# Seven chunks instead of three gather raw rows, and 13 blocks of normalised rows are turned in three rounds, in a two-layer graph network on Trainium2

## The chip, the cores and the metric

The kernel runs on one core of a Trainium2 chip. The metric is the device time of one launch in microseconds (us), taken as the median of several runs; lower is better. The core has TensorE (PE, with PEld for its weight loads), VectorE (DVE), ScalarE (ACT), GpSimd (POOL) and SyncE (SP), and 16 DMA engines that all of them issue to.

## The reference

A graph of 6250 nodes with 128 features each has 106250 edges (50000 random pairs in both directions and a loop for each node), sorted by destination. Two transformer convolutions with two heads of 64 run after each other; all of it is in f32. The features of an edge, `e`, come from a cosine time encoding (32) and a message (64).

```python
kj    = k[src] + e                            # k, q, v: linear maps of h
alpha = einsum('ehc,ehc->eh', q[dst], kj) / sqrt(C)
a     = softmax of alpha over the edges of one dst
conv(h) = segment_sum((v[src] + e) * a, dst) + h @ Ws + bs

h = conv1(x)
h = relu(batchnorm(h))                        # mean and variance over all 6250 nodes
out = layernorm(x + conv2(h))
```

The batch norm stands between the layers: its mean and variance are complete only when layer 1 has given its last rows. Per feature it becomes a scale and a shift.

## The kernel before

**Tiling.** The edges are cut into `NC` = 105 chunks of up to 1024 edges (`T` = 8 tiles of 128), each for at most 64 consecutive destinations. A chunk's features lie in a tile `ff` (an edge per partition and tile). The feature rows of its sources are fetched by eight indirect DMAs of 128 rows each, issued by GpSimd (`gather`, L752): from `xv_d` in layer 1, and in layer 2 from one of two tables in DRAM. `h_d` holds the raw rows of layer 1's result, `hn_d` the same rows after batch norm and relu.

**Layers.** `conv(c, extra, first_blocks)` runs once for each layer (c = 0 and 1), as one loop over rounds k from -4 to 107 with the order of instructions written out by hand (L948 and on). Every engine works through its own instructions in that order and waits for the others by semaphores. Round k issues, in this order:

- `fetch(k+4)`: SP loads the messages (`fmsg`), the tables of scores (`ftab`) and, in layer 2, the encodings (`fz`), their turned copies (`fxT<-et_d`) and the residual rows (`fr`); then `gather(k+4)` on GpSimd.
- `score(k, 0)` (L831, L832), `turn_weights(k-1)` (L856 on TensorE, copied by ScalarE at L857), `divide(k-2)` on VectorE (L868 to L871), `score(k, 1)`, `lowest(k)` (L838, L840), `finish_turn(k-2)` (TensorE turns the divided sums, L883 and L884; VectorE copies them, L886).
- `turn_in(k+1, 0)`: TensorE turns half of the next chunk's rows (L806), ScalarE copies the result out of PSUM: in layer 2 with scale, shift and relu if the rows are raw (L811), as they are otherwise (L813).
- `gather_sums(k-1)`: eight matmuls (L863) that sum the weighted rows by destination, the last readers of the chunk's `ff`. Then `weigh(k)` (ScalarE, L846), `turn_in(k+1, 1)`, `apply(k-2)` (L899, L900 in layer 2), and `settle(k+2)`, a copy of messages.
- `pull(extra)`: a step or two of work from a generator. In layer 2 these are, for one block of 512 nodes after the other, the tables of scores (L630 on TensorE, copied by ScalarE and VectorE) and the residual `x + h @ Ws + bs` (L1093).
- `finish(k-2)`, `normalise(k)` if the chunk's rows are raw, the copy of the encodings into `ff` (L997), and the store of results.

**Buffers.** `ff` has six, `fmsg` three, `fz` four; so the gather of chunk k+6 can begin only when the sums (L863) of chunk k are done. PSUM has three banks for everything that is turned (tag "tr", with the blocks of nodes below), three for scores, one for sums and one for results. The tiles of rows on their way to DRAM (`fhr`, `fxr`) share three buffers.

**Raw rows.** A chunk k < `RAW` in layer 2 gathers from `h_d`, which is complete when layer 1 is. Its turned rows get scale, shift and relu from ScalarE on the way out of PSUM (L811); the untransposed rows, which L863 needs, get them on VectorE:

```python
def normalise(k):
    rows = ch[k].f[:, :, 1:1 + D]
    for i, op in enumerate((OP.mult, OP.add)):                 # L876
        nc.vector.tensor_tensor(rows, rows, pl.spread[:, None, i].to_broadcast([P, T, D]), op)
    nc.vector.tensor_scalar(rows, rows, 0.0, None, op0=OP.max) # L877
```

All later chunks gather from `hn_d` and need none of this, but the first of them must wait until all of `hn_d` is stored.

**Between the layers.** VectorE forms scale and shift from the statistics (L1067 to L1077), ScalarE does the relu of the first block of `hT` (the 6250 nodes as columns, in SBUF), the tables and the residual of that block are made, and scale and shift are spread over all partitions (L1122 to L1128). Then `conv(1, ...)` begins. In its first round, k = -4, right after `fetch(0)` and `gather(0)`, it calls `first_blocks`: ScalarE does relu of blocks 1 to 12 in place (L1107), and for each of the 13 blocks TensorE turns four tiles of 128 nodes (L1028), VectorE copies them out of PSUM (L1030) and SP stores them to `hn_d` (L1038; the last block is 106 rows and goes in two stores, L1043; 14 stores in all).

Of the kernel before, what the change touches and what calls it, by code (L numbers as in the profile page):

```python
# [7 lines left out]
F32 = mybir.dt.float32  # L8
# [5 lines left out]
P = 128  # L14
# [4 lines left out]
TD = 32  # L19
# [3 lines left out]
GE = GT * P  # L23
# [21 lines left out]
T = 8  # L45
# [618 lines left out]
def ordered(ctx: ExitStack, tc: tile.TileContext, pl, x, dst, edge_attr_64, conv2, bn_g, bn_b, out):  # L664
# [3 lines left out]
    N = x.shape[0]  # L668
# [19 lines left out]
    def first(k):  # L688
        return max(0, N - NN * (NC - k)), min(N - 1 if k == NC - 1 else N - NN, NN * k)
# [6 lines left out]
    AHEAD = 4  # L696

    SINGLE = 40

    RAW = 3  # L700

    def conv(c, extra, first_blocks=None):

# [2 lines left out]
        load = cs.enter_context(tc.tile_pool(name=f"fload{c}", bufs=AHEAD + 2))  # L706
# [16 lines left out]
        def fetch(k):  # L723
            s = ch[k] = Plan()
            lo, hi = first(k)
            s.nb = nc.sync.value_load(pl.nbs[0:1, k:k + 1], min_val=lo, max_val=hi)
            sl = nc.sync.value_load(pl.sls[0:1, k:k + 1], min_val=0, max_val=E - CE)
            s.f = f = load.tile([P, T, FW], F32, name="ff")
            s.msg = load.tile([P, T, MSG], F32, name="fmsg", bufs=3)
            nc.sync.dma_start(s.msg, edge_attr_64[bass.ds(sl, CE), :].rearrange("(p t) d -> p t d", t=T))  # L730
            if c:
                nc.vector.memset(f[:, :, D + EW:1 + D + EW], 1.0)
            else:
                bits = small.tile([P, T, BITS], I32, name="fbits")
                nc.vector.tensor_tensor(bits, pl.dsts[:, :, k:k + 1].to_broadcast([P, T, BITS]),
                                        pl.bitm[:, None, :].to_broadcast([P, T, BITS]), OP.bitwise_and)
                nc.vector.tensor_scalar(f[:, :, D + EW:D + EW + BITS], bits, 0.0, None, op0=OP.is_equal)
                nc.vector.tensor_copy(f[:, :, D + EW + BITS:], bits)
            s.tab = load.tile([P, NN * H, 3 - c], F32, name="ftab")
            nc.sync.dma_start(s.tab, pl.tab_d[c][:, bass.ds(s.nb, NN)].rearrange("p n h w -> p (n h) w"))  # L740
            if c:
                s.z = load.tile([P, T, TD], F32, name="fz", bufs=AHEAD)
                nc.sync.dma_start(s.z, enc_d[k].rearrange("p (t d) -> p t d", d=TD))
                s.et = ets[k % len(ets)]
                nc.sync.dma_start(s.et, et_d[k])
                s.r = load.tile([NN, D], F32, name="fr", bufs=AHEAD + 3)
                nc.sync.dma_start(s.r, res_d[bass.ds(s.nb, NN), :])

        def gather(k):
            f = ch[k].f  # L750
            ch[k].rows = [
                nc.gpsimd.indirect_dma_start(  # L752
                    out=f[:, t, (1 if c else 0):1 + D], out_offset=None, in_=(h_d if k < RAW else hn_d) if c else pl.xv_d,
                    in_offset=bass.IndirectOffsetOnAxis(ap=pl.srcs[:, t, k:k + 1], axis=0))
                for t in range(T)]
# [24 lines left out]
        def sine():  # L780
            arg, *of = args
            args.clear()
            z = work.tile([P, 2, T, TD], F32, name="fzs")
            nc.scalar.activation(z[:, :len(of)], arg[:, :len(of)], AF.Sin, bias=qpi)
            turned.extend((k, z[:, i]) for i, k in enumerate(of))
# [11 lines left out]
        def turn_in(k, u):  # L797
# [7 lines left out]
            for t in range(4):  # L805
# [3 lines left out]
                s.rows = []  # L809
            if c and k < RAW:  # L810
                nc.scalar.activation(s.ft[:, u * GE:(u + 1) * GE], px, AF.Relu, bias=pl.shift, scale=pl.scale)  # L811
# [11 lines left out]
        def score(k, u):  # L823

            s = ch[k]
            if u == 0:
                s.ps = []
            ps = p_s.tile([P, GE], F32, name="fps")
            s.ps.append(ps)
            w = slice(u * GE, (u + 1) * GE)  # L830
            nc.tensor.matmul(ps, s.tab[:, :, 0], s.ft[:, w], start=True, stop=False)  # L831
            nc.tensor.matmul(ps, s.tab[:EC, :, 1], s.et[:, w], start=False, stop=True)  # L832
# [110 lines left out]
        def pull(gen, n):  # L943
            for _ in range(n):
                next(gen, None)

        with cs, tc.manual_schedule():
            for k in range(-AHEAD, NC + 3):  # L948
                def on(j):
                    return 0 <= j < NC  # L950

                if on(k + AHEAD):
                    fetch(k + AHEAD)
                    gather(k + AHEAD)
                if k == -AHEAD and c:
                    first_blocks()
                if on(k):
                    score(k, 0)
                if on(k - 1):
                    turn_weights(k - 1)  # L960
                place()
                if on(k - 2):
                    divide(k - 2)
                if on(k):
                    score(k, 1)
                if on(k):
                    lowest(k)
                if on(k - 2):
                    finish_turn(k - 2)
                if on(k + 1):  # L970
                    turn_in(k + 1, 0)
                if on(k - 1):
                    gather_sums(k - 1)
                if on(k):
                    weigh(k)
                if on(k + 1):
                    turn_in(k + 1, 1)
                if on(k - 2):
                    apply(k - 2)
                if on(k + 2):  # L980
                    settle(k + 2)
                for j in (k + 2,) if k < SINGLE else (k + 2, k + 3) if k == SINGLE else (k + 3,):
                    if c == 0 and on(j):
                        encode(j)
                        if j < SINGLE + 3:
                            sine()
                if k >= 0:
                    at_round[0] = k
                    pull(extra, 2 if k < 4 or k > 96 else 1)
                if on(k - 2):  # L990
                    finish(k - 2)
                if len(args) == 3 or args and k == NC - 4:
                    sine()
                if c and on(k):
                    if k < RAW:
                        normalise(k)
                    nc.vector.tensor_copy(ch[k].f[:, :, 1 + D:1 + D + TD], ch[k].z)  # L997
                for _ in range(min(len(done), 2 if k > NC - 12 else 1)):
                    store(*done.pop(0))
            at_round[0] = 2 * NC  # L1000
            for _ in extra:
                pass
            for rows in done:
                store(*rows)


    NT = NP // GE

    with tc.tile_pool(name="fpw", bufs=2) as pw:
# [96 lines left out]
            r = slice(b0 * GE, (b0 + 1) * GE)  # L1106
            nc.scalar.activation(hT[:, r], hT[:, r], AF.Relu, bias=shift, scale=scale)  # L1107

        def first_blocks():

            for b0 in range(1, NT):
                relu(b0)
            for b0 in range(-(-N // GE)):
                put_rows(hn_d, b0, turned_rows(b0))

        with tc.tile_pool(name="fpp2", bufs=3, space=bass.MemoryType.PSUM) as pp, tc.manual_schedule():
# [262 lines left out]
```

## Time and profile before

| | before |
|---|---|
| time, median of 3 runs | 2705.21 us (2699.31 to 2705.34) |
| the profiled execution: its own time | 2727.81 us |
| its span in the trace | 2725.5 us |
| instructions | 38782 |
| VectorE, ScalarE, GpSimd busy | 49%, 45%, 59% of the span |
| gathers of layer 1 and layer 2 (L752) | 840 of 958 ns and 840 of about 951 ns |
| moved by DMA | 393.39 MB, mean 144 GB/s |

The times come from the chip's profiler, from one execution; the runs that give the median are others. An engine is busy when one of its instructions executes; waiting, register and DMA-issuing instructions don't count. In the lists of instructions, "x" is a count of equal instructions in a row, and the brackets hold the idle time of that engine before the instruction and what ended it: another instruction or a transfer by its tile, "issue" where the trace shows nothing that it waited for, "remote" where the event that released it has no work of this core's trace beside it. An arrow `out<-in` names the tile written and the tiles read, and what stands before "L" and a number is the engine, after it the line of the kernel.

### The profile page before, as it was taken

How to read it: one execution, taken by the hardware profiler on the slowest of the kernel's cores; microseconds unless marked ns; L12 is line 12 of the kernel's file. 1: busy time of each engine (PE TensorE's matmuls, PEld its weight loads, DVE VectorE, ACT ScalarE, POOL GpSimd, SP SyncE). 2: the span in 40 equal slices, each digit the busy share in tenths (PEclk: the TensorE clock that was granted, in tenths of full speed). 3: DMA queues.
4: the chain of work that ended last, by engine and by line, in shares of the span. 5: the costliest groups of instructions: out<-in, count | busy, mean ns of one | idle time of the engine just before them, and what ended most of it. 6: DMA issues, size and time to landing. Idle time of an engine off the chain costs nothing. (4 is left out here: it accounts for less than half of the span.)

```text
span 2725.5 us, 38782 instructions
## 1 busy us (share of the span) xinstructions
PE 2315.9 (85%) x11482; PEld 1703.1 (62%) x11482; DVE 1332.0 (49%) x4144; ACT 1231.3 (45%) x2147; POOL 1608.2 (59%) x1701
## 2 busy tenths in 40 slices
PE   4599899999898888888956888888988888988887
PEld 3366666667666666666734666666666666656655
DVE  5266666666666666666634333333333333333333
ACT  2266666665554555545522333333333343433344
POOL 3466666566666666666336666666666666666660
PEclk8699999999999999999978999999999999999999
DMA  6255555445544455445436554545555555554440
GB/s 204 76 152 161 160 151 162 123 150 158 161 150 136 150 161 159 143 142 145 127 107 175 157 152 132 160 143 156 155 144 146 159 151 147 150 140 129 139 132 29
DMA packets 239223, 393.39 MB, mean 144 GB/s; under 512 B 62049, under 2 KB 156893, under 8 KB 235677
## 3 DMA queue, kind: packets, MB, share of 16 engines
q1 hardware_dynamic: 166302, 237.60, 28.5%
q0 software_dynamic: 54144, 112.01, 16.2%
q10 hardware_dynamic: 18558, 41.20, 4.1%
q8 instruction: 97, 1.59, 0.2%
q14 instruction: 122, 0.99, 0.1%
HBM read 274.66 MB, written 112.55 MB: 142 GB/s over the span
## 5 line engine op out<-in xcount | busy, mean ns | idle before, releaser
L752 POOL DMA_INDIRECT ff<-xv_d,fsrcs x840 | 804.8, 958 | 511.9 <-issue 212.4
L752 POOL DMA_INDIRECT ff<-hn_d,fsrcs x816 | 775.8, 951 | 466.0 <-issue 208.0
L813 ACT COPY fft<-fpx 128x512 f32<-128x512 f32 x414 | 243.7, 589 | 1124.5 <-remote 459.8
L863 PE MATMUL fpa<-ff,fpt 128*128 128x225 f32 x3360 | 677.4, 354 | 3.5 <-issue 3.5
L863 PEld LDWEIGHTS fpa<-ff,fpt 128*128 128x128 f32 x3360 | 621.6, 190 | 8.0 <-issue 4.7
L838 DVE TENSOR_REDUCE flow<-fps 128x1 f32<-128x512 f32 x420 | 283.4, 686 | 516.7 <-PE fpx L806 167.9
L831 PE MATMUL fps<-fft,ftab 128*128 128x512 f32 x840 | 473.5, 647 | 46.3 <-ACT fft L813 34.5
L856 PEld LDWEIGHTS fppt<-fident,fs 128*128 128x128 f32 x1680 | 200.5, 145 | 145.8 <-issue 75.8
L857 ACT COPY fpt<-fppt 128x512 f32<-128x512 f32 x420 | 227.6, 585 | 119.9 <-issue 46.1
L846 ACT ACTIVATE fs<-fps,fm 128x512 f32<-128x512 f32 x420 | 266.6, 689 | 5.7 <-DVE fm L840 3.3
L806 PE MATMUL fpx<-fident,ff 128*128 128x128 f32 x1680 | 256.2, 276 | 9.4 <-issue 5.0
L856 PE MATMUL fppt<-fident,fs 128*128 128x128 f32 x1680 | 233.7, 283 | 13.0 <-ACT fft L811 5.5
L831 PEld LDWEIGHTS fps<-fft,ftab 128*128 128x128 f32 x840 | 168.0, 234 | 107.4 <-ACT fft L813 53.4
L832 PE MATMUL fps<-fet,ftab 112*128 112x512 f32 x420 | 220.4, 606 | 16.7 <-issue 16.7
L832 PE MATMUL fps<-fxT,ftab 112*128 112x512 f32 x420 | 230.8, 632 | 2.5 <-DMA fxT<-et_d 2.5
L806 PEld LDWEIGHTS fpx<-fident,ff 128*128 128x128 f32 x1680 | 200.6, 142 | 40.5 <-issue 27.6
L818 PE MATMUL fpe<-fident,ff 128*112 128x128 f32 x840 | 131.5, 280 | 60.9 <-ACT fft L813 54.7
L886 DVE COPY fat<-fpo 128x256 f32<-128x256 f32 x210 | 88.4, 421 | 177.6 <-remote 66.6
L832 PEld LDWEIGHTS fps<-fet,ftab 112*128 112x128 f32 x420 | 105.8, 252 | 95.5 <-issue 93.6
L832 PEld LDWEIGHTS fps<-fxT,ftab 112*128 112x128 f32 x420 | 89.5, 213 | 114.1 <-issue 109.4
L819 ACT COPY fet<-fpe 112x512 f32<-112x512 f32 x210 | 126.1, 601 | 55.2 <-remote 17.6
L818 PEld LDWEIGHTS fpe<-fident,ff 128*112 128x112 f32 x840 | 93.7, 135 | 78.3 <-ACT fft L813 69.1
(217 smaller groups left out, 2382.7 us busy)
## 6 DMA issues: line engine op xcount, KB each, us to landing
fmsg<-in_edge_attr SPq DMA_DIRECT2D x210, 256.0 KB
et_d<-fet SPq DMA_DIRECT2D x105, 448.0 KB
fxT<-et_d SPq DMA_DIRECT2D x105, 448.0 KB
ftab<-tab_d SPq DMA_DIRECT2D x105, 192.0 KB
tab_d<-fo ACTq DMA_DIRECT2D x13, 1536.0 KB
ff<-xv_d,fsrcs POOLq DMA_INDIRECT x840
enc_d<-fzs SPq DMA_DIRECT2D x105, 128.0 KB
ftab<-tab_d SPq DMA_DIRECT2D x105, 128.0 KB
```

The source lines that it names most:

```text
L752: nc.gpsimd.indirect_dma_start(out=f[:, t, (1 if c else 0):1 + D], out_offset=None, in_=(h_d if k < RAW else hn_d) if c else pl.xv_d, in_o ...
L806: turn = nc.tensor.transpose(px[:, t * P:(t + 1) * P], s.f[:, u * 4 + t, 1:1 + D], ident)
L813: nc.scalar.copy(s.ft[:, u * GE:(u + 1) * GE], px)
L818: nc.tensor.transpose(pe[:EC, t * P:(t + 1) * P], s.f[:, u * 4 + t, 1 + D:], ident)
L819: nc.scalar.copy(s.et[:, u * GE:(u + 1) * GE], pe[:EC])
L831: nc.tensor.matmul(ps, s.tab[:, :, 0], s.ft[:, w], start=True, stop=False)
L832: nc.tensor.matmul(ps, s.tab[:EC, :, 1], s.et[:, w], start=False, stop=True)
L838: nc.vector.tensor_reduce(low[:, u:u + 1], s.ps[u], AX.X, OP.min)
L846: nc.scalar.activation(s.s[:, u * GE:(u + 1) * GE], s.ps[u], AF.Exp, bias=s.bias, scale=-1.0)
L856: nc.tensor.transpose(pp[:, t * P:(t + 1) * P], s.s[:, at:at + P], ident)
L857: nc.scalar.copy(s.pt[:, u * GE:(u + 1) * GE], pp)
L863: nc.tensor.matmul(s.pa, s.pt[:, t * P:(t + 1) * P], s.f[:, t, 1:1 + D + EW], start=t == 0, stop=t == T - 1)
```

## The change

`RAW` goes from 3 to 7: chunks 0 to 6 gather from `h_d` and are normalised on the fly, and chunk 7 is the first to gather from `hn_d`. `first_blocks` no longer runs at the start of layer 2. It takes the round as its argument and is called at the end of rounds 0, 1 and 2, ahead of the pulled work: four relus each (blocks 4k+1 to 4k+4), and then the blocks 0 to 4 in round 0, 5 to 8 in round 1 and 9 to 12 in round 2 are turned, copied and stored. The gather of chunk 7 is issued at the start of round 3, behind these stores. The encodings `fz` get a fifth buffer.

```diff
-    RAW = 3
+    RAW = 7
...
-                s.z = load.tile([P, T, TD], F32, name="fz", bufs=AHEAD)
+                s.z = load.tile([P, T, TD], F32, name="fz", bufs=AHEAD + 1)
...
                 if on(k + AHEAD):
                     fetch(k + AHEAD)
                     gather(k + AHEAD)
-                if k == -AHEAD and c:
-                    first_blocks()
                 if on(k):
                     score(k, 0)
...
+                if c and k in range(3):
+                    first_blocks(k)
                 if k >= 0:
                     at_round[0] = k
                     pull(extra, 2 if k < 4 or k > 96 else 1)
...
-        def first_blocks():
-
-            for b0 in range(1, NT):
+        def first_blocks(k):
+
+            for b0 in range(4 * k + 1, 4 * k + 5):
                 relu(b0)
-            for b0 in range(-(-N // GE)):
+            for b0 in range(4 * k + (k > 0), 4 * k + 5):
                 put_rows(hn_d, b0, turned_rows(b0))
```

## The prediction

> **What bounds the kernel now.** I read the busy times of the engines first, then the same busy times by stretches of time, then the instructions in order of time where the stretches look unlike the rest. The columns of the stretches are the stretch, its length, busy time (and instructions) of TensorE, weight loads, VectorE, ScalarE and GpSimd, the granted TensorE clock, the DMA share and GB/s.
>
> ```profile
> PE 2315.9 (85%) x11482; PEld 1703.1 (62%) x11482; DVE 1332.0 (49%) x4144; ACT 1231.3 (45%) x2147; POOL 1608.2 (59%) x1701
> ...
> 1400.00:1420.00 20.00, 3.76 (x20) 2.72 (x20) 1.79 (x3) 2.31 (x4) 15.09 (x16) 0.63 0.53 153
> ...
> 1437.80:1455.00 17.20, 14.54 (x49) 8.80 (x47) 7.13 (x14) 7.08 (x9) 13.17 (x14) 0.80 0.70 192
> 1455.00:1472.60 17.60, 4.46 (x6) 1.71 (x6) 0.51 (x2) 2.06 (x4) 9.99 (x11) 0.73 0.28 88
> ...
> 1600.00:1700.00 100.00, 87.49 (x445) 63.36 (x443) 36.23 (x118) 34.18 (x75) 62.22 (x66) 0.97 0.51 148
> ```
>
> TensorE is the busiest engine, 87 of 100 us in a steady stretch of layer 2. Between the layers it is not: it works 3.8 us of the 20 from 1400, and 4.5 us of the 17.6 from 1455. The change acts on this stretch alone. The order of time there (start, length, engine, line, and in brackets the idle time before and what ended it):
>
> ```profile
> 1390.05 0.94 POOL L752 DMA_INDIRECT ff<-h_d,fsrcs  x1 [58.19 <-DVE fshift L1077]
> ...
> 1400.47 1.53 PE L1028 MATMUL fpg<-fident,fhT 128*128 128x128 f32 x12 [0.59 <-DVE fspread L1128]
> ...
> 1406.43 0.69 DVE L1030 COPY fhr<-fpg 128x512 f32<-128x512 f32 x1 [6.02 <-issue]
> ...
> 1413.41 0.69 DVE L1030 COPY fhr<-fpg 128x512 f32<-128x512 f32 x1 [6.28 <-remote]
> ...
> 1418.76 0.94 POOL L752 DMA_INDIRECT ff<-h_d,fsrcs  x1 [0.30 <-issue]
> 1421.81 0.69 DVE L1030 COPY fhr<-fpg 128x512 f32<-128x512 f32 x1 [7.71 <-remote]
> ...
> 1432.01 0.66 PE L806 MATMUL fpx<-fident,ff 128*128 128x128 f32 x4 [0.58 <-DMA hn_d<-fhr]
> ...
> 1437.87 0.94 POOL L752 DMA_INDIRECT ff<-hn_d,fsrcs  x1 [18.17 <-DMA hn_d<-fhr]
> ...
> 1452.57 0.69 DVE L838 TENSOR_REDUCE flow<-fps 128x1 f32<-128x512 f32 x1 [2.81 <-remote]
> ...
> 1462.50 0.78 ACT L811 ACTIVATE fft<-fpx,fshift,fscale 128x512 f32<-128x512 f32 x1 [14.94 <-issue]
> ...
> 1467.09 0.94 POOL L752 DMA_INDIRECT ff<-hn_d,fsrcs  x1 [0.30 <-issue]
> ...
> 1472.47 0.78 ACT L811 ACTIVATE fft<-fpx,fshift,fscale 128x512 f32<-128x512 f32 x1 [8.04 <-remote]
> ...
> 1472.65 0.94 POOL L752 DMA_INDIRECT ff<-hn_d,fsrcs  x1 [4.61 <-remote]
> ...
> 1484.60 0.94 POOL L752 DMA_INDIRECT ff<-hn_d,fsrcs  x1 [1.80 <-PE fpo L900]
> ...
> 1496.72 1.11 POOL L752 DMA_INDIRECT ff<-hn_d,fsrcs  x1 [2.20 <-PE fpx L806]
> ```
>
> Three things are to be seen. The gathers of chunks 0 to 2 run without a break, one every (1418.76 - 1390.05) / 23 = 1.248 us; chunk 3 waits until 1437.87 for the last stored block; chunk 6 starts at 1472.65, chunk 7 at 1484.60, and then a chunk takes 12.1 us. Second, chunk 0's rows lie there from about 1390.05 + 8 x 1.248 = 1400, but TensorE turns them at 1432.01, behind the 13 blocks. Third, the blocks are not slow by their own work: three blocks' transposes were issued by 1402.0, and VectorE takes them up at 1406.4, 1413.4 and 1421.8, that is 7.0 and 8.4 us apart. The last of these is the first after the gathers ended. While gathers run for long, TensorE's results reach the other engines late; I call that holding. Between 1452.57, 1462.50 and 1472.47 it is again 9.9 and 10.0 us, late in the second run of gathers (chunks 3 to 5, 1437.87 to 1468.03). What causes it the profile does not say. It is there in the start of layer 1 too, where six chunks are gathered without a break, as layer 2 will do after the change:
>
> ```profile
> 40.53 0.96 POOL L752 DMA_INDIRECT ff<-xv_d,fsrcs  x1 [25.40 <-PE fpx L654]
> ...
> 69.00 0.58 ACT L813 COPY fft<-fpx 128x512 f32<-128x512 f32 x1 [6.76 <-remote]
> ...
> 80.14 0.58 ACT L819 COPY fet<-fpe 112x512 f32<-112x512 f32 x1 [10.55 <-remote]
> ...
> 91.34 0.58 ACT L813 COPY fft<-fpx 128x512 f32<-128x512 f32 x1 [10.62 <-remote]
> ...
> 99.32 0.94 POOL L752 DMA_INDIRECT ff<-xv_d,fsrcs  x1 [0.30 <-issue]
> ...
> 101.83 0.58 ACT L819 COPY fet<-fpe 112x512 f32<-112x512 f32 x1 [9.91 <-issue]
> ...
> 109.86 1.91 PE L630 MATMUL fpg<-fxT,fm 128*128 128x512 f32 x2
> ...
> 125.08 0.97 POOL L752 DMA_INDIRECT ff<-xv_d,fsrcs  x1 [24.82 <-PE fpa L863]
> ```
>
> There a result is taken up every 10.5 to 11.2 us until the gathers stop at 100.3, and chunk 6 follows 24.8 us after that.
>
> **The change, part by part.** I count to the gathers of chunks 6 and 7 and the sums (L863) that free their buffers, since from there on a chunk costs 12.1 us in both kernels.
>
> *Blocks leave the front.* 49 transposes, 13 copies, 12 relus and 14 stores go; TensorE can turn chunk 0 at about 1402 instead of 1432.0, 30 us earlier. SP no longer has 14 stores between the loads of chunk 0 and those of chunks 1 to 4.
>
> *Raw rows for seven chunks.* Six feature buffers let chunks 0 to 5 be gathered in one run: 1390.05 + 48 x 1.248 = 1450.0. TensorE has rows from 1400 on, but holding starts about then: at 8.4 us a result (the same place, the value nearest to the middle of 7.0 and 11.2) 48 us pass 5.7 results. Chunk 0 needs two turned halves and two score halves, chunk 1 two turned halves: six. So at 1450 chunk 0 is scored and chunk 1 nearly turned; layer 1 is at that point at 109.86 and starts chunk 6 at 125.08, 15.2 us later. If nothing were held it would be done long before 1450; if 11.2 held, two results are missing and layer 1's whole 24.8 us apply.
>
> *Blocks at the ends of rounds 0, 1, 2* (five, four, four). The nearest rows:
>
> ```profile
> L1107 ACT ACTIVATE fhT<-fhT,fshift,fscale 128x512 f32<-128x512 f32 x13 | 9.5, 799 | 2.2 <-DVE fdiag L1126 1.3 <-DVE fshift L1077 0.8
> ...
> L1030 DVE COPY fhr<-fpg 128x512 f32<-128x512 f32 x12 | 8.1, 690 | 24.3 <-remote 14.0 <-issue 6.0 <-DMA hn_d<-fhr 2.8
> ...
> 1424.65 2.34 DMA hn_d<-fhr
> ...
> 2669.61 3.21 PE L863 MATMUL fpa<-ff,fpt 128*128 128x225 f32 x16
> ...
> 2678.90 3.21 PE L863 MATMUL fpa<-ff,fpt 128*128 128x225 f32 x16
> ```
>
> Four copies are 4 x 0.69 = 2.8 us; with three buffers and 2.34 us until a store lands, (0.69 + 0.39 + 2.34) / 3 = 1.14 us a block, 4.6 us for four; four relus 3.2 us on ScalarE ahead of the table copies and of the next round's turned weights. A round's blocks so cost 2.8 to 4.6 us; beside the gathers' gap they might cost nothing. I take 3, for round 0's five 4. Chunk 6 then starts at 1450.0 + 15.2 + 4 = 1469.2, 3.5 us earlier than 1472.65. Round 1 takes 12.1 + 3: its sums are done at 1484.3, 0.3 earlier than 1484.60. Round 2 adds 3.
>
> *Chunk 7 waits for the last block.* Before, its gather needs only the free buffer. Now POOL also waits for round 2's stores, which come behind four relus (3.2), the last copy (0.7) and the landing (2.3) and some transposes: 7 us, from 5.5 to 10. Behind that wait stand all later gathers; TensorE waits for none of them for three rounds. While POOL stands still a round is faster: at the end of layer 2, where nothing is gathered, 2678.90 - 2669.61 = 9.3 us instead of 12.1, which gives back up to 2.8; I take 2.4. The 7 us late gathers are absorbed by the three chunks that lie ready, or, since a steady round is 8 x 1.248 = 10.0 us of gathers and a gap, not made good at all: 0 to 6.7, I take the half, 3.4.
>
> *Four more chunks normalised on VectorE.*
>
> ```profile
> 1475.15 1.32 POOL L752 DMA_INDIRECT ff<-hn_d,fsrcs  x1 [0.30 <-issue]
> ...
> 1487.43 2.48 DVE L876 TENSOR_TENSOR ff<-ff,fspread 128x1024 f32<-128x1024 f32 x2
> ...
> 1489.95 0.69 DVE L877 TENSOR_SCALAR ff<-ff 128x1024 f32<-128x1024 f32 x1
> ...
> 1491.77 0.30 PE L883 MATMUL fpo<-fident,fa 128*128 128x128 f32 x1 [2.51 <-issue]
> ```
>
> 2.48 + 0.69 = 3.17 us a chunk, in rounds 3 to 6. VectorE has the time (36 of 100 us busy), but the division of the chunk before is queued behind it, and TensorE's L883 behind that: it stood 2.51 us in such a round. Four rounds cost 0 to 12.7 us; I take half of 2.51 each, 5.0. A gather beside L876 took 1.32 instead of 0.94, 1.5 us for four, which is within that.
>
> The Trainium skill ("SBUF — State Buffer", section "Who interferes with whom") says that a tensor_scalar in a two-port mode shuts GpSimd out for the whole instruction, and that descriptor generation is not hindered by tensor_tensor. By that rule the four L877 would hold POOL up to 4 x 0.69 = 2.8 us and L876 nothing; the row above shows a gather stretched beside L876. The sum would be 1.3 us higher by the rule, and I keep the row.
>
> *At no cost:* the fifth buffer for the encodings only lets SP's load go earlier, and the relu of raw rows on ScalarE (L811, 0.78 us) instead of a copy (0.58) is hidden by ScalarE's idle time (34 of 100 us busy).
>
> Sum, against the profiled execution (span 2725.5, 2727.8 with what lies around it): -0.3 (sums of chunk 1) + 3 (round 2's blocks) - 2.4 + 3.4 + 5.0 = +8.7, so 2736.5 in a profile. The median of the runs, 2705.2, lies 22.6 us below the profiled execution; I put the same difference on it: 2714.
>
> **The rivals.**
>
> *Faster: TensorE's results aren't held when it has real work.* For it: from 1437.80 to 1455 it was busy 14.5 of 17.2 us beside gathers. Against it: layer 1's start. Then it gains the 30 us of the front, pays 13 blocks at 1.0 us in the rounds and 1.5 us of stretched gathers: -15, 2690. It decides if the sums of chunk 0 are done before 1450.
>
> *No change.* Gathers set the pace; the normalising and the late chunk 7 are hidden: -0.3 + 3 - 2.4 = 0, 2705 to 2706. For it: VectorE's low share. Against it: the 2.51 us wait.
>
> *Slower by more: holding comes a second time.* After the wait, chunks 7, 8 and 9 are gathered in one run, 30 us, as 3 to 5 are before, and that run ends in a stretch of 17.6 us with 4.5 us of TensorE work: 13 us lost on top of 9, 2727. Against it: the buffer of chunk 9 may not be free in time, which breaks the run.
>
> **How the numbers follow.** Forecast +9 with its own range of +4 to +16 (2709 to 2721): 0.42. Faster 0.25, no change 0.18, holding twice 0.15. A measurement can tell about 0.3%, 8 us, from no change. Of the forecast 0.30 lies above that and 0.12 within; of the faster case 0.24 is beyond it; of the twice held one 0.14. This gives slower 0.45, same 0.31, faster 0.24. The range reaches into the faster and the twice held case: 2687 to 2729.
>
> **What would show it.** In the changed kernel's profile: the raw gathers run unbroken from 1390 to 1450; ScalarE's first relu of turned rows starts before 1412, and after it results come 7 to 11 us apart; the sums of chunk 0 fall between 1460 and 1470 (before: 1450.3); chunk 6's gather at 1465 to 1473; chunk 7's at 1488 to 1495 with a wait on the stores in front of it; L883 stands 1 to 3 us in rounds 3 to 6. Wrong it would be if the sums of chunk 0 come before 1450 (the faster rival), or if chunk 7 starts before 1484.6.

## The result, and the profile after

The changed kernel takes 2735.6 us (median of 4 runs, 2727.8 to 2739.1) against 2702.4 us (2699.3 to 2705.3) for the kernel before: a ratio of 1.0108 with an interval of 1.0093 to 1.0124, so some 29 us slower by the ratio (the two medians are 33 us apart). A second set of runs (after2, below) gave 1.0115 (1.0093 to 1.0137). The profiled execution after took 2734.05 us, its span is 2732.3 us.

The profile of before that the prediction worked with, 2727.8 us, does not belong beside these: it lies 22 us above the longest of the runs before. Chips differ by as much: over those that the runs below met, the kernel before has medians of 2701 to 2734 us (and of 2291 on one, last section). A second profile of before, the run b0 (2705.4 us), stands for it here. The table counts from the start of layer 1's last sums (first L863 of its last chunk) to the starts of the sums of chunks of layer 2, in us, from the traces:

| chunk of layer 2 | profile before | b0 | changed |
|---|---|---|---|
| start of layer 1's last sums in the span | 1375.8 | 1366.5 | 1366.4 |
| 0 | 74.5 | 71.3 | 101.4 |
| 1 | 103.8 | 101.9 | 119.9 |
| 2 | 117.1 | 115.2 | 137.9 |
| 6 | 162.2 | 161.0 | 190.5 |
| 10 | 210.3 | 208.2 | 233.5 |
| 20 | 330.1 | 327.1 | 353.3 |
| 50 | 694.8 | 686.3 | 710.7 |
| 104, the last | 1329.4 | 1313.8 | 1344.1 |

So against b0 18 us are lost before chunk 1 and 11.5 more by chunk 6 (190.5 - 161.0 = 29.5); 4 come back by chunk 10, and from there on the distance is 24 to 30. The first line of the page and the stretches of the junction after (columns as in the prediction):

```profile
PE 2316.6 (85%) x11482; PEld 1708.9 (63%) x11482; DVE 1346.4 (49%) x4156; ACT 1234.8 (45%) x2147; POOL 1605.0 (59%) x1701
```

```profile
1404.70:1435.00 30.30, 0.00 (x0) 0.00 (x0) 1.53 (x4) 4.85 (x7) 22.97 (x25) 0.57 0.39 109
1435.00:1460.60 25.60, 5.85 (x18) 3.54 (x18) 2.65 (x4) 2.06 (x3) 4.38 (x5) 0.50 0.45 127
...
1500.00:1510.00 10.00, 7.04 (x31) 6.36 (x32) 4.88 (x12) 1.93 (x3) 7.51 (x8) 0.66 0.63 177
1600.00:1700.00 100.00, 89.06 (x427) 63.56 (x426) 36.85 (x122) 38.00 (x79) 65.06 (x69) 0.93 0.50 141
```

TensorE's total is as before, and so is the steady stretch. But for 30 us it does nothing, and for the next 25.6 it works 5.9 us at half its clock. The instructions there, in order of time:

```profile
1380.71 0.94 POOL L752 DMA_INDIRECT ff<-h_d,fsrcs  x1 [58.00 <-ACT fstd L1071]
...
1395.35 1.63 ACT L811 ACTIVATE fft<-fpx,fshift,fscale 128x512 f32<-128x512 f32 x2 [8.51 <-issue]
...
1403.20 1.04 PE L806 MATMUL fpx<-fident,ff 128*128 128x128 f32 x8
...
1404.22 0.68 DVE L838 TENSOR_REDUCE flow<-fps 128x1 f32<-128x512 f32 x1
...
1407.42 0.70 SPq L740 DMA_DIRECT2D ftab<-tab_d  x1
...
1410.97 0.69 DVE L838 TENSOR_REDUCE flow<-fps 128x1 f32<-128x512 f32 x1 [6.07 <-remote]
...
1422.27 0.78 ACT L811 ACTIVATE fft<-fpx,fshift,fscale 128x512 f32<-128x512 f32 x1 [25.30 <-remote]
...
1433.47 0.78 ACT L811 ACTIVATE fft<-fpx,fshift,fscale 128x512 f32<-128x512 f32 x1 [7.86 <-remote]
...
1439.66 0.94 POOL L752 DMA_INDIRECT ff<-h_d,fsrcs  x1 [0.30 <-issue]
1444.76 0.69 DVE L1030 COPY fhr<-fpg 128x512 f32<-128x512 f32 x1 [17.08 <-remote]
...
1448.77 0.34 SPq L740 DMA_DIRECT2D ftab<-tab_d  x1
...
1454.78 6.99 SPq L1038 DMA_DIRECT2D hn_d<-fhr  x5
1459.92 1.45 DVE L1030 COPY fhr<-fpg 128x512 f32<-128x512 f32 x2 [10.34 <-DMA hn_d<-fhr]
1460.67 2.08 PE L630 MATMUL fpg<-fhT,fm 128*128 128x512 f32 x2 [8.75 <-DVE fhr L1030]
...
1471.31 0.94 POOL L752 DMA_INDIRECT ff<-h_d,fsrcs  x1 [30.70 <-PE fpa L863]
...
1498.64 2.49 DVE L876 TENSOR_TENSOR ff<-ff,fspread 128x1024 f32<-128x1024 f32 x2
...
1499.84 0.94 POOL L752 DMA_INDIRECT ff<-hn_d,fsrcs  x1 [18.84 <-PE fps L832]
...
1502.45 0.45 DVE L871 TENSOR_SCALAR fa<-fpa,finv 128x225 f32<-128x225 f32 x1
...
1502.96 0.47 PE L883 MATMUL fpo<-fident,fa 128*128 128x128 f32 x1 [3.80 <-DMA ff<-hn_d,fsrcs]
```

TensorE has turned and scored chunk 0 and turned chunk 1 by 1404.2 (1403.20 + 1.04). ScalarE takes up the second half of chunk 1 at 1433.47. The results come at 1410.97, 1422.27, 1433.47 and 1444.76, that is 11.3, 11.2 and 11.3 us apart: holding, as the prediction calls it. It ends with the 48 gathers, at 1440.6 and one result more. Then round 0's stores go out only at 1454.78, the last two copies wait for a free row buffer until 1459.92, and TensorE until 1460.67. The gather of chunk 6 starts 1471.31 - 1440.60 = 30.7 us after the run ended.

In b0 the same happens at two other places, in the 13 blocks and late in the second run of gathers:

```profile
1410.20 0.69 DVE L1030 COPY fhr<-fpg 128x512 f32<-128x512 f32 x1 [6.35 <-remote]
...
1426.90 0.95 POOL L752 DMA_INDIRECT ff<-hn_d,fsrcs  x1 [16.31 <-DMA hn_d<-fhr]
...
1461.27 0.78 ACT L811 ACTIVATE fft<-fpx,fshift,fscale 128x512 f32<-128x512 f32 x1 [17.84 <-remote]
...
1461.44 0.94 POOL L752 DMA_INDIRECT ff<-hn_d,fsrcs  x1 [3.85 <-remote]
1462.10 1.97 PE L856 MATMUL fppt<-fident,fs 128*128 128x128 f32 x8 [16.93 <-ACT fft L811]
```

### The profile page after: what moved, and what is told of

Its sections match the earlier page's. It is cut to its first block, busy times and chain, and to the rows that moved or that the text cites. A ratio compares the mean times of both kernels' runs of the same rounds, so it can differ in the third digit from the quotient of the medians.

```text
span 2732.3 us, 38868 instructions
## 1 busy us (share of the span) xinstructions
PE 2316.6 (85%) x11482; PEld 1708.9 (63%) x11482; DVE 1346.4 (49%) x4156; ACT 1234.8 (45%) x2147; POOL 1605.0 (59%) x1701
## 5 line engine op out<-in xcount | busy, mean ns | idle before, releaser
L752 POOL DMA_INDIRECT ff<-hn_d,fsrcs x784 | 746.0, 952 | 438.6 <-issue 200.5
L863 PE MATMUL fpa<-ff,fpt 128*128 128x225 f32 x3360 | 682.9, 356 | 0.7 <-issue 0.6
L863 PEld LDWEIGHTS fpa<-ff,fpt 128*128 128x128 f32 x3360 | 626.7, 192 | 6.1 <-issue 1.7
L831 PE MATMUL fps<-fft,ftab 128*128 128x512 f32 x840 | 466.8, 638 | 65.7 <-issue 37.6
L806 PEld LDWEIGHTS fpx<-fident,ff 128*128 128x128 f32 x1680 | 202.3, 143 | 41.1 <-issue 30.3
L818 PEld LDWEIGHTS fpe<-fident,ff 128*112 128x112 f32 x840 | 94.8, 136 | 76.6 <-ACT fft L813 69.0
L777 DVE SCALAR_TENSOR_TENSOR farg<-fturns,farg 128x256 f32<-128x256 f32 x315 | 134.1, 426 | 10.8
```

The lines of the kernel that those rows point to most:

```text
L752: nc.gpsimd.indirect_dma_start(out=f[:, t, (1 if c else 0):1 + D], out_offset=None, in_=(h_d if k < RAW else hn_d) if c else pl.xv_d, in_o ...
L777: nc.vector.scalar_tensor_tensor(arg, turn, -part, arg, op0=OP.mult, op1=OP.add)
L806: turn = nc.tensor.transpose(px[:, t * P:(t + 1) * P], s.f[:, u * 4 + t, 1:1 + D], ident)
L818: nc.tensor.transpose(pe[:EC, t * P:(t + 1) * P], s.f[:, u * 4 + t, 1 + D:], ident)
L863: nc.tensor.matmul(s.pa, s.pt[:, t * P:(t + 1) * P], s.f[:, t, 1:1 + D + EW], start=t == 0, stop=t == T - 1)
```

## The experiments

The theory after the result: the run of 48 gathers holds results to its end, the moved blocks win nothing in front of it, and round 0's stores stand behind late loads in SP's queue. The rival: the blocks in the rounds and the normalises are dear by themselves. Each set of runs was on one chip with the kernel before on it; ratios, with intervals, are to that. The last two columns are from each run's profile, in us after layer 1's last sums as in the table above, and a profile is one execution.

| run | before, us | run, us | ratio | chunk 1 | chunk 10 |
|---|---|---|---|---|---|
| b0 | 2701.2 | 2704.1 | 1.0004 (0.9992 to 1.0016) | 101.9 | 208.2 |
| raw7_front | 2701.2 | 2719.6 | 1.0053 (1.0032 to 1.0074) | 114.1 | 221.6 |
| acts | 2701.2 | 2734.5 | 1.0115 (1.0095 to 1.0136) | 115.0 | 229.3 |
| paced | 2701.2 | 2720.5 | 1.0068 (1.0045 to 1.0090) | 95.2 | 224.9 |
| paced_acts | 2729.8 | 2739.8 | 1.0039 (1.0023 to 1.0056) | 88.2 | 222.6 |
| norm3 | 2729.8 | 2752.1 | 1.0084 (1.0064 to 1.0103) | 121.9 | 236.8 |
| nowait7 | 2729.8 | 2755.5 | 1.0103 (1.0082 to 1.0125) | 120.0 | 233.0 |
| bpaced | 2729.8 | 2734.9 | 1.0021 (1.0008 to 1.0033) | 80.2 | 221.3 |
| bp2 | 2733.5 | 2811.7 | 1.0275 (1.0228 to 1.0323) | 78.7 | 195.3 |
| ap2 | 2733.5 | 2830.1 | 1.0347 (1.0304 to 1.0390) | 85.7 | 221.4 |
| catch4 | 2703.5 | 2712.9 | 1.0035 (1.0020 to 1.0049) | 80.1 | 203.2 |
| catch3 | 2703.5 | 2730.2 | 1.0099 (1.0075 to 1.0122) | 78.7 | 195.5 |
| bbreak | 2703.4 | 2710.7 | 1.0024 (1.0014 to 1.0034) | 85.2 | 217.2 |
| abreak | 2703.4 | 2708.8 | 1.0016 (1.0002 to 1.0030) | 81.2 | 214.0 |
| catch34 | 2703.8 | 2711.2 | 1.0029 (1.0007 to 1.0052) | 76.6 | 192.8 |
| c3a | 2291.4 | 2311.4 | 1.0083 (1.0070 to 1.0097) | 81.1 | 175.8 |
| c3b | 2291.4 | 2309.4 | 1.0075 (1.0061 to 1.0089) | 77.8 | 173.8 |
| after2 | 2705.4 | 2736.0 | 1.0115 (1.0093 to 1.0137) | 119.4 | 233.7 |

**b0**, the kernel before once more.

> The kernel before once more, for a second profile of it. Theory A (the profiled execution of before was slow in its steady rounds, by chance, and the junction of the layers there is typical): 2700 to 2706 us, rounds of layer 1 and 2 at about 12.1 and 11.85 us, and still about 210 us from the last sums (L863) of layer 1 to those of chunk 10 of layer 2. Rival B (the junction itself was slow in that execution): the same time, steady rounds as before (12.2 and 12.05 us), and the 210 us shrink to about 195 to 200.

A was right about the junction (208.2), and layer 1's rounds took 12.14 and layer 2's 11.89 us where the first profile has 12.21 and 12.05.

**raw7_front**: seven raw chunks with the blocks where they were.

```diff
-    RAW = 3
+    RAW = 7
-                s.z = load.tile([P, T, TD], F32, name="fz", bufs=AHEAD)
+                s.z = load.tile([P, T, TD], F32, name="fz", bufs=AHEAD + 1)
```

> RAW = 7 and the fifth fz buffer alone, the 13 blocks at the start of layer 2 as before. Theory A (the unbroken run of 48 gathers is what costs, since TensorE's results reach the other engines only every 11.2 us until it ends): the 13 blocks are not done until the gathers end, the sums of chunk 0 come 100 us or more after the last sums of layer 1 (before: 74.5), and the time is 2735 to 2750. Rival B (the blocks in rounds 0 to 2 are what costs, through their copies and stores): 2705 to 2715.

Neither: 102.4 us to chunk 0 as A said, yet half of the loss (0.0053 of 0.0108). The copies of blocks, and what follows the end of the run at 1442.45:

```profile
1418.48 0.69 DVE L1030 COPY fhr<-fpg 128x512 f32<-128x512 f32 x1 [9.11 <-remote]
...
1428.98 0.69 DVE L1030 COPY fhr<-fpg 128x512 f32<-128x512 f32 x1 [9.81 <-remote]
...
1440.19 0.69 DVE L1030 COPY fhr<-fpg 128x512 f32<-128x512 f32 x1 [10.52 <-issue]
1447.88 0.69 DVE L1030 COPY fhr<-fpg 128x512 f32<-128x512 f32 x1 [7.00 <-remote]
...
1455.09 1.69 ACT L811 ACTIVATE fft<-fpx,fshift,fscale 128x512 f32<-128x512 f32 x2 [60.30 <-PE fpx L806]
```

ScalarE takes up chunk 0's turned rows 58 us later than in the changed kernel (1455.09 - 1368.4 = 86.7 us after layer 1's last sums, against 1395.35 - 1366.4 = 29.0), and its sums still come at 102.4 us against 101.4. The 30 us that the moved blocks should free at the front are not there. The long run costs 12.2 us at chunk 1 (114.1 - 101.9); moving the blocks then adds 5.8 at chunk 1, 11.0 at chunk 2 (137.9 against 126.9) and 14.8 at chunk 6 (190.5 against 175.7).

**acts** and **paced**: `nc.scalar.dma_start` for the stores of `hn_d`; and the gathers of chunks 2 to 5 taken out of the run, each behind an instruction of TensorE.

```diff
+                if c and k == 0:
+                    gather(2, last[0])     # behind score(0, 1)
                 if on(k):
                     lowest(k)
...
+                if c and k == 1:
+                    gather(4, last[0])     # behind gather_sums(0)
                 if on(k + 1):
                     turn_in(k + 1, 1)
+                if c and k in (0, 1):
+                    gather(3 if k == 0 else 5, last[0])
```

> The changed kernel with the 14 stores of hn_d issued from ScalarE's queue instead of SP's. Theory A (in round 0 the stores stand in SP's queue behind loads, so VectorE's copies wait 10.3 us for the three row buffers and TensorE 8.8 us): the wait falls below 3 us, the sums of chunk 0 come about 8 us earlier, and the time is 2725 to 2729. Rival B (the copies are late because TensorE's results are, and the stores only follow): 2733 to 2738, as the changed kernel.

> The changed kernel with its first long run of gathers broken up: the gather of chunk 2 waits for the last score matmul of chunk 0, that of chunk 3 for chunk 1's last turned half, that of chunk 4 for chunk 0's last sums and that of chunk 5 for chunk 2's last turned half. Theory A (holding comes with a long unbroken run of gathers): no result of TensorE is taken up 7 to 11 us late any more, the sums of chunk 0 come 55 to 65 us after the last sums of layer 1 (the changed kernel: 101.4), those of chunk 10 at most 215 us after (233.5), and the time is 2705 to 2718. Rival B (holding does not come from the run of gathers, or the gathers bound the front by themselves): the sums of chunk 0 may be earlier, but chunk 10 stays at 230 us or more and the time at 2732 or above.

In acts:

```profile
1446.54 3.68 PE L1028 MATMUL fpg<-fident,fhT 128*128 128x128 f32 x16 [38.32 <-ACT fhT L1107]
...
1454.34 1.69 PE L630 MATMUL fpg<-fhT,fm 128*128 128x512 f32 x2 [2.64 <-DVE fhr L1030]
```

The 8.75 us wait shrinks to 2.64, as A said, and the profiled execution, which was the lowest of the four at 2723, has chunk 1 4.9 us earlier (115.0); but TensorE stands 38 us in front of it, and the median shows no gain over the changed kernel, as B said. In paced:

```profile
1402.39 0.94 POOL L753 DMA_INDIRECT ff<-h_d,fsrcs  x1 [2.92 <-PE fps L836]
...
1402.60 0.78 ACT L815 ACTIVATE fft<-fpx,fshift,fscale 128x512 f32<-128x512 f32 x1 [6.70 <-PE fps L836]
...
1409.35 1.88 DVE L1041 COPY fhr<-fpg 128x512 f32<-128x512 f32 x3
...
1427.67 6.61 SPq L1049 DMA_DIRECT2D hn_d<-fhr  x5
1432.50 1.38 DVE L1041 COPY fhr<-fpg 128x512 f32<-128x512 f32 x2 [21.27 <-DMA hn_d<-fhr]
1433.25 2.08 PE L630 MATMUL fpg<-fhT,fm 128*128 128x512 f32 x2 [19.42 <-DVE fhr L1041]
```

One pause of 2.9 us in the gathers, and the first three blocks are copied at 1409 instead of 1445 to 1449. Then the stores do stand in SP's queue, behind the loads of two chunks, for 16 us, and TensorE stands 19.4. Chunk 1 comes 24.7 us earlier than in the changed kernel; by chunk 10 a run of 24 gathers (1445 to 1475) and the blocks have taken back 16 of that (224.9 against 233.5 leaves 8.6). The time falls, against B, but A's numbers are all missed: 76.5 us to chunk 0 (at most 65), 224.9 to chunk 10 (215), 2720.5 us (2718).

**paced_acts, norm3, nowait7**: both edits together; no normalise for chunks 3 to 6; no wait of chunk 7 on the stores.

```diff
-                    if k < RAW:
+                    if k < 3:                                  # norm3
                         normalise(k)
...
-                    ... in_=(h_d if k < RAW else hn_d) if c else pl.xv_d,
+                    ... in_=h_d if c else pl.xv_d,             # nowait7
```

> The broken-up gathers of the run paced, and the stores of hn_d on ScalarE's queue. In paced VectorE's copies of round 0 waited 21.3 us for stores that stood in SP's queue behind the loads of two chunks, and TensorE 19.4 us behind them. Theory A (two causes: results held during a long run of gathers, and stores queued behind SP's loads): with both gone no wait of TensorE in the junction is above 6 us, the sums of chunk 0 come 55 to 63 us after the last sums of layer 1 (paced 76.5), those of chunk 10 at most 213 us after (224.9), and the time is 2700 to 2711. Rival B (the stores wait as long in ScalarE's queue, or the gathers bound the rounds by themselves): chunk 10 at 220 us or more, time 2716 to 2724.

> The changed kernel without normalise for chunks 3 to 6, whose rows L863 then sums raw (part of the computation is left out). Theory A (the division stands behind it in VectorE's queue): 4 to 6 us less than the changed kernel, 2729 to 2732, taken out of rounds 3 to 6. Rival B (hidden, the rounds are bound by gathers and late results): 2734 to 2737.

> The changed kernel with all chunks of layer 2 gathering from h_d, so that chunk 7 waits for no store (the rows from chunk 7 on are not normalised: part of the computation is left out). Theory A (the gather of chunk 7, about 10 us late, delays the chunks behind it by a third to a half): the gather of chunk 7 starts at the end of chunk 1's sums, chunk 10's sums come 3 to 5 us earlier than the changed kernel's 233.5, time 2729 to 2732. Rival B (the chunks that lie ready absorb it): chunk 10 within 1.5 us of 233.5, time 2734 to 2737.

paced_acts falls to 1.0039, between the theories: chunk 1 is 7 us earlier again, but it still has runs of 16 and 24 gathers, and chunk 10 gains only 2.3. norm3: from chunk 2 to chunk 7 it takes 61.2 us (201.7 - 140.5) where the changed kernel takes 62.8; the ratios are 0.0024 or 6.5 us apart (1.0084 against 1.0108), and their intervals overlap. So these runs don't tell the price of the four normalises from nothing. nowait7: the gather of chunk 7 starts 10 us earlier,

```profile
1497.92 0.94 POOL L752 DMA_INDIRECT ff<-h_d,fsrcs  x1 [8.88 <-PE fpa L863]
```

1497.9 - 1374.5 = 123.4 us after layer 1's last sums against 1499.8 - 1366.4 = 133.4, and chunk 10 comes at 233.0 against 233.5. That is rival B's number: the chunks that lie ready absorb it. The changed kernel was not profiled on this chip, and ratios of 1.0103 and 1.0108 can't show or exclude the 3 to 5 us of theory A.

**bpaced, bp2, ap2**: the kernel before (bpaced, bp2) and the changed one (ap2) with other places for the gathers of layer 2; ap2 has the stores of `hn_d` on ScalarE's queue too.

```diff
+        paced = {(0, 0): 2, (1, 0): 3, (2, 0): 4, (2, 1): 5, (3, 0): 6, (4, 0): 7, (4, 1): 8}   # bpaced
+        paced = {(k, 0): k + 2 for k in range(NC - 2)}                                      # bp2
...
+                if c and (k, 0) in paced:
+                    gather(paced[k, 0], last[0])               # behind score(k, 1)
```

> The kernel before (RAW = 3, the blocks at the front) with the gathers of chunks 1 to 8 issued later: chunk 1 behind the turning of block 5, chunks 2, 3, 4, 6 and 7 behind the score matmuls of the chunk that many rounds on, 5 and 8 at the ends of rounds 2 and 4; from chunk 9 on as before. Theory A (held results cost the kernel before 25 to 35 us too: 16.9 us of TensorE's idle time in one gap and 17 us among the blocks): the sums of chunk 0 come 55 to 63 us after the last of layer 1 (71.3), chunk 1 at most 78 (101.9), chunk 10 at most 190 (208.2), time 2672 to 2688. Rival B (with gathers only two chunks ahead the rows come late, and what the front wins the rounds lose): chunk 10 at 205 us or more, time 2698 or above.

> The kernel before, layer 2 gathering two chunks ahead instead of four: chunk 1 behind the turning of block 5, every later chunk k+2 behind the score matmuls of chunk k, so that no run is longer than the eight gathers of a chunk (the run bpaced still had runs of 16 and 24, and each ended in TensorE waiting 14.8 and 16.5 us). Theory A (results are held from about 10 us into a run): no wait of TensorE above 6 us in the junction, the sums of chunk 10 at most 198 us after the last of layer 1 (the kernel before: 208 to 210), the time 0.992 to 0.997 of the kernel before. Rival B (two chunks ahead is too few, rows come late in every round): rounds of layer 2 at 12.3 us or more, 1.005 or above.

> The changed kernel with the same order of gathers (two chunks ahead in layer 2, chunk 1 behind chunk 0's last turned half) and the stores of hn_d on ScalarE's queue. Theory A (the changed kernel loses by its run of 48 gathers and by the stores behind SP's loads, and what is left are the blocks in three rounds and four normalises, 10 to 17 us as the two kernels of the second set of runs stood to each other): no wait of TensorE above 6 us in the junction, chunk 10's sums at most 210 us after the last of layer 1 (233.5), time 0.996 to 1.001 of the kernel before. Rival B (two chunks ahead is too few): rounds of layer 2 at 12.3 us or more, 1.010 or above.

bpaced has chunk 1 22 us earlier than b0, and loses it, as rival B said, in two places where its gathers catch up in longer runs. In the second, chunks 5, 6 and 7 are gathered in one run, from 1497.22 to 1527.00:

```profile
1497.22 0.95 POOL L756 DMA_INDIRECT ff<-hn_d,fsrcs  x1 [8.01 <-PE fpo L891]
...
1511.73 0.59 ACT L864 COPY fpt<-fppt 128x512 f32<-128x512 f32 x1 [7.57 <-remote]
...
1520.86 0.59 ACT L864 COPY fpt<-fppt 128x512 f32<-128x512 f32 x1 [8.54 <-issue]
...
1526.05 0.94 POOL L756 DMA_INDIRECT ff<-hn_d,fsrcs  x1 [0.30 <-issue]
1528.57 0.69 DVE L845 TENSOR_REDUCE flow<-fps 128x1 f32<-128x512 f32 x1 [21.89 <-remote]
```

The round there takes 28.5 us, those around it 10 to 15. A run of 24 holds results further into the layer too, some rounds behind the last of the 13 blocks and its stores. bp2 has almost no such run and reaches chunk 10 in 195.3 us, 13 earlier than b0; then two chunks ahead prove too few (rounds of 13.19 us), so both theories were right on their parts. ap2 shows such rounds too (13.10 us).

ap2 beside bp2 answers the rival that blocks and normalises are dear by themselves. Both gather two chunks ahead, and neither has a run of more than 16 at the junction; they differ in the change, in the queue of the stores and in what chunk 1's gather waits for. ap2 is still 18 us slower by the medians. Its sums of chunk 0 come no earlier (64.5 us against 63.4), those of chunk 3 17.8 us later (124.1 against 106.3), those of chunk 6 23.9 and those of chunk 10 26.1. So here the moved blocks gain nothing at the front, and they and chunk 1's later gather cost 5 to 6 us in each of the first three steps. In the order of instructions, five of the 13 blocks still stand in front of chunk 0's sums, at the end of round 0.

**catch4, catch3, bbreak, abreak, catch34**: the catching up spread over rounds (catch4, catch3, catch34, of before), or three and five pauses alone (bbreak of before, abreak of the changed kernel with the stores on ScalarE's queue).

```diff
+                    gather_to(T * (k + 2) + 5 + extra_rows(k - 1), last[0])   # catch4: behind score(k, 1)
...
+                    gather_to(T * (k + 3) + extra_rows(k), last[0])           # behind the sums
...
+        paced = {(1, 1): 4, (2, 0): 5, (2, 2): 6}                             # bbreak
+        paced = {(0, 0): 2, (0, 3): 3, (1, 1): 4, (2, 0): 5, (2, 3): 6}       # abreak
```

> The kernel before, layer 2 starting two chunks ahead as in the run bp2, but each round up to 16 issues one gather of 128 rows more (five behind the second score matmuls, four behind the sums), until the gathers are four chunks ahead; from round 17 on the order of before. Theory A (bp2 won the junction, 195 us to chunk 10 against 208 to 210, and lost only by staying two chunks ahead): chunk 10's sums at most 199 us after the last of layer 1, chunk 20's at most 321 (the kernel before: 327 to 330), rounds of 11.9 to 12.1 us after that, time 0.993 to 0.998 of the kernel before. Rival B (while it catches up GpSimd hardly pauses, so results are held and the win is lost): chunk 20 at 327 us or later, time 1.000 or above.

> As catch4, but only eight gathers are caught up, so that from round 8 on the gathers are three chunks ahead, five of each chunk behind the score matmuls and three behind the sums. Theory A (three chunks are enough): chunk 20's sums at most 321 us after the last of layer 1, rounds of 11.8 to 12.1 us, time 0.992 to 0.999. Rival B (the waits on TensorE's score matmuls in each round cost by themselves): rounds at 12.4 us or more, time 1.010 or above.

> The kernel before with three gathers moved: chunk 4 behind the sums of chunk 0, chunk 5 behind the score matmuls of chunk 2, chunk 6 behind chunk 3's last turned half; all else, four chunks ahead from round 4 on, as before. Theory A (the second run of 24 gathers of the kernel before costs it TensorE's wait of 16.9 us): that wait falls below 7 us, the sums of chunk 1 come at most 92 us after the last of layer 1 (101.9), those of chunk 10 at most 202 (208.2), time 0.995 to 0.999 of the kernel before. Rival B (the wait comes from something else at this place, or the later gathers of chunks 4 to 6 cost as much as they win): chunk 10 at 207 us or later, time 1.000 or above.

> The changed kernel, stores of hn_d on ScalarE's queue, and five gathers moved: chunk 2 behind the score matmuls of chunk 0, chunk 3 behind round 0's last block, chunk 4 behind the sums of chunk 0, chunk 5 behind the score matmuls of chunk 2, chunk 6 behind round 2's last block. Theory A (29 us are 12 to 18 of held results and late stores and the rest blocks in three rounds and normalises): the sums of chunk 1 come at most 90 us after the last of layer 1 (the changed kernel 119.9, the kernel before 101.9), chunk 10 at most 216 (233.5), time 1.000 to 1.004 of the kernel before. Rival B (the blocks and the normalises are the larger part by themselves): chunk 10 at 222 us or later, time 1.006 or above.

> The kernel before with layer 2's gathers two chunks ahead at first, three from round 8 to round 20 (as catch3, which had chunk 20's sums 318 us after the last of layer 1 and then rounds of 12.28 us), and from round 21 on four chunks ahead in the order of before. Theory A (catch3 lost its win only by the waits it kept in every later round): chunk 20 at most 321 us (the kernel before 327), chunk 50 at most 684 (686.3), rounds of 11.9 us from there on, time 0.996 to 1.000 of the kernel before. Rival B (the step to four ahead gives the win back): chunk 50 at 690 or later, time 1.002 or above.

abreak shows the most. With the work of the changed kernel and its stores on another queue, five pauses bring it from 1.0108 to 1.0016, from 29 us to 4, with chunk 1 at 81.2 us instead of 119.9, as theory A said; so 25 of the 29 us go with the order of gathers and the queue of the stores. It does not show that the moved blocks cost only 4 us: the kernel before that it is measured against has held stretches of its own (chunk 1 at 101.9 us in b0, 78.7 in bp2), and beside bp2 the change cost 18. bbreak's wait of 16.9 us is gone (chunk 1 at 85.2) and yet it is slower than before: a run of 24 gathers follows at 1464. Each of the catch runs won the front and gave it back: catch4 in rounds of 13.2 us while it catches up, catch3 in rounds of 12.28 us, catch34 (319.3 at chunk 20, 8 us ahead) in the run of 24 with which it steps to four ahead (452.4 at chunk 30, 7 behind). In the time, rival B was right of bbreak, catch4 and catch34, and catch3 lies between the theories. No version beat the kernel before.

**c3a, c3b, after2**: three chunks ahead to the end with one wait a round, on the sums; and the changed kernel again.

> As catch34 up to round 20; from round 21 on the gather of chunk k+3 stands at the start of round k and waits for the sums of chunk k-2, so that it stays three chunks ahead. Theory A (the win can be kept with one wait a round): chunk 20 at most 321 us after the last sums of layer 1, chunk 50 at most 682 (686.3), rounds of 11.9 us, time 0.995 to 1.000 of the kernel before. Rival B (three chunks ahead cost in each round): rounds at 12.1 us or more from round 20 on, time 1.003 or above.

> As c3a, with the step to one wait a round at round 9 instead of 21. Theory A: chunk 20 at most 319 us after the last sums of layer 1, time 0.994 to 0.999 of the kernel before. Rival B: rounds at 12.1 us or more from round 9 on, time 1.003 or above.

> The changed kernel again, beside the kernel before on the same chip. Theory A (its cost is results held in a run of 48 gathers, with the stores that are late behind them): where the kernel before takes 2690 us or more, 1.009 to 1.013 of it, and the sums of chunk 0 come about 101 us after the last of layer 1; where it takes about 2290 us (no holding), 0.990 to 1.000 of it and chunk 0's sums at most 60 us after. Rival B (the cost is in the blocks and the normalises): 1.008 to 1.015 on either chip.

c3a and c3b are slower than before, as rival B said of the time, but on a chip where rounds are 10 us and nothing is held (below), so they don't answer the question. after2 repeats the result on a usual chip, chunk for chunk, which both theories allow there.

## Why the prediction was wrong

- **The direction was right and the size was not**: 9 us forecast, 29 measured. The parts that the sum names were at work, but the largest error is in its smallest term: the -0.3 us at chunk 1's sums came out as +16 against the profile that the sum was made from (119.9 against 103.8 us), +18 against b0. The next two points say why.
- **Raw gathers in one unbroken run, results 7 to 11 us apart, chunk 0 scored and chunk 1 nearly turned at its end**: right, in part by luck. The run was as long as forecast (59.9 us). Results came 11.2 us apart and not 8.4, but holding began later than the prediction had it: chunk 0's turned rows were still taken up at once (1395.35), and the first late result is that at 1410.97. The two errors cancel in the count of results.
- **15.2 us, as in layer 1, plus 4 us for round 0's blocks until chunk 6 is gathered**: here the forecast failed. 30.7 us against 19.2, which makes 11.5 of the 20 us that were missed. The blocks were priced by their own work, 4 us; in fact TensorE got past them 20 us after the run had ended (1460.67 - 1440.60), since relu, copies and stores of round 0 all stand behind the held results, and the stores behind SP's loads as well. The prediction counted a gain of SP's loads from the 14 stores that leave, and not the stores' own place behind the loads of chunks 3 and 4.
- **3 us for the blocks of a round, -2.4 us for a round without gathers**: mis-sized. The sums of chunk 1 came 18.5 us after those of chunk 0 (forecast 15.1), and those of chunk 2 another 18.0 us later (12.7): 3.4 and 5.3 us more. No faster round was seen while GpSimd stood. What the way to chunk 2's sums took besides is in the rows: L883 waits 3.80 us, and the granted clock is 0.66 from 1500 to 1510. The row puts that wait down to a gather, but L871, which writes the `fa` that L883 reads and stands behind the normalise at 1498.64, ended at 1502.90, just before it.
- **+3.4 us for chunk 7's late gather**: the gather was late, by 10 us rather than 7, and no loss is seen by chunk 10 (0.5 us in nowait7).
- **+5.0 us for four normalises**: not settled. L883 stands behind the four of them for 0.80, 1.53, 2.53 and 2.04 us, nearly the 1 to 3 us forecast, but norm3 can't tell what that costs.
- **The base**: the profile of before lay 22.6 us above the median, and I took that difference over to the changed kernel. Its own profile lies at its median. The forecast of 2736.5 for the profiled execution and the 2734.05 measured agree by chance.
- **The rivals**: holding came only once, chunks 7 and 8 were gathered with a pause between them. Results were held, so the faster rival did not apply. The +13 us that this rival of a second holding stood for are matched in size by what moving the blocks added by chunk 6, 14.8 us.

The rule of the Trainium skill cited in the prediction ("SBUF — State Buffer", "Who interferes with whom") would have L877 hold GpSimd and L876 not. The changed kernel's trace disagrees, as before's did:

```profile
1512.22 2.49 DVE L876 TENSOR_TENSOR ff<-ff,fspread 128x1024 f32<-128x1024 f32 x2
1512.67 1.60 POOL L752 DMA_INDIRECT ff<-hn_d,fsrcs  x1 [0.31 <-issue]
...
1514.57 0.99 POOL L752 DMA_INDIRECT ff<-hn_d,fsrcs  x1 [0.30 <-DMA ff<-hn_d,fsrcs]
1514.74 0.69 DVE L877 TENSOR_SCALAR ff<-ff 128x1024 f32<-128x1024 f32 x1
```

The gather beside L876 took 1.60 us, the one beside L877 0.99. Not every gather beside L876 is stretched: the one at 1499.84 above, inside the L876 from 1498.64 to 1501.13, took 0.94. What stretches one is open.

## What to carry to other kernels

Moving work out of the way of an engine wins only if the engine's results get out and the work does not stand in front of the next thing that counts: look first for what sets the end of the stretch, here the end of a run of gathers that the same change made twice as long, and the blocks in front of chunk 0's sums. Try a cure on the kernel before as well: pauses in the gathers helped both kernels at the front. Price moved work with everything queued ahead of it on each queue it uses, stores included, and not by its own length. And take a second profile of the kernel before making a sum against one execution.

## What the runs showed of the hardware

Where results are held, the first late one is taken up some 15 to 30 us into an unbroken run of gathers (1410.97 - 1380.71 = 30.3 in the changed kernel, 1511.73 - 1497.22 = 14.5 in bpaced). One result of TensorE then gets through in 6 to 11 us, and it is over 2 to 8 us after the run ends. Most of SP's issues take 0.70 us then, and 0.33 to 0.49 otherwise. One of the seven chips of the experiments did not do this at all, in the profiles of c3a and c3b: there the kernel before takes 2291 us instead of 2701 to 2734. In c3a's steady rounds on it, beside the same stretch of b0 (the first row is c3a's),

```profile
1600.00:1700.00 100.00, 97.78 (x518) 72.47 (x517) 42.68 (x146) 46.20 (x97) 75.90 (x80) 1.00 0.64 181
```

```profile
1600.00:1700.00 100.00, 85.15 (x443) 61.86 (x442) 36.47 (x119) 33.34 (x75) 63.12 (x67) 1.00 0.59 158
```

TensorE is busy 97.8 us of 100 against 85.2, at the same granted clock of 1.00, gathers run for 990 us without a pause, and a round takes 10.05 us, both layers alike in this (10.54 us in layer 1 against 12.14; layer 1 is the same code in both runs, layer 2 is not). If holding is all that sets the chips apart, which no run shows by itself, it takes 1.6 to 1.8 us of every steady round on the others, an estimate from these rounds. Why chips differ, what in a gather delays the results, and what the changed kernel does on such a chip stay open; it was not tried there.
